# Another order of the pieces within one period of a software-pipelined graph network on one core

## The chip, the core and the metric

The kernel runs on one core of one Trainium2 chip. TensorE (PE) multiplies matrices into PSUM, of which the kernel uses eight banks; VectorE (DVE), ScalarE (ACT) and GpSimd (POOL) do the elementwise work; SyncE (SP) issues the DMA transfers. Each engine works through its own queue in order, and semaphores make one engine wait for another. The metric is the device time in microseconds of one launch, lower is better.

## What is computed

64 graphs of 256 nodes with 256 features, all in fp32, through two layers. `adj` holds 0 and 1. Layer 0 is graph attention (twice), LayerNorm, and a feed-forward block with relu:

```python
def _gat(h, adj, W, a, out_features):          # twice
    Wh = h @ W
    e = leaky_relu(Wh @ a[:out] + swap(Wh @ a[out:]), 0.2)
    return softmax(where(adj > 0, e, NEG), axis=1) @ Wh
h = _layernorm(x + _gat(_gat(x, adj, W1, a1), adj, W2, a2), g_ln1, b_ln1)
x = _layernorm(h + relu(h @ w_ff1 + b_ff1) @ w_ff2 + b_ff2, g_ln2, b_ln2)
```

Layer 1 is attention with 8 heads whose weights are split by relation, then LayerNorm and a feed-forward block with gelu (256 to 1024 to 256, as in layer 0):

```python
attn = softmax(q @ k.T / sqrt(32))
for r in range(4):
    out = out + (attn * (adj == r)) @ (x @ Wv[r] + bv[r])
x = _ln(x + out @ Wo + bo, g1, beta1)
return _ln(x + gelu(x @ W1 + b1) @ W2 + b2, g2, beta2)
```

## The kernel before

**Pieces.** `binary` (L211) does all the work; `general` (L1181) stands behind a test at the end and handles adjacency values other than 0 and 1, which this input doesn't have. For each graph `graph` (L1126) fills a table of small functions, the *pieces*, of one to 64 instructions each. Their names have a stage and a step:

- L: loads of one graph. L.xT (columns of x), L.adj (L363) and L.x (rows of x, L373), 256 KB each.
- G, graph attention (`gat`, L824): projections wh0, wh1 on TensorE and their copies wc0, wc1 on ScalarE; for each of the two steps A and B the transposed targets e, terms lr, masked maximum ad (L893 to L899, VectorE), exponentials ex, normalisation rz; the products gA0, gA1 with copies wd0, wd1, and the second product gB. Then LayerNorm A: lnA, rsA, nmA.
- F: the features of layer 0's first LayerNorm are turned into columns (dtA on VectorE, dmA and mgA on SP, see below), feed-forward block, LayerNorm B (lnB, rsB, nmB), columns again (dtB, dmB, mgB), and the queries and keys.
- A: the values of layer 1, scores sc0, sc1, maxima mx, exponentials ex, reciprocals rz, normalisation sp (POOL), the turning of the weights over DRAM (dt, dm, mg), masks pm (L1071, VectorE), products o0, o1 and their copies oc0, oc1.
- T: the output projection wo, LayerNorm C, the second feed-forward block, LayerNorm D, and the store T.out.
- S and W occur at the start alone (weights, and matmuls that warm up TensorE).

**Seven products.** A product of 2 x 2 blocks is done with seven block products instead of eight (`seven_products`, L692). It appears four times for each graph: h, the hidden layer of a feed-forward block (`into`, L758); f, its output (`out_of`, L796); q, queries and keys (L967); v, values (L991). TensorE's part is five pieces: `a` (products X and Z, two PSUM banks), `b` (Y, a third bank), `c` (adds to X and to Y), `d` and `e` (add to X). The running values of X are taken out between them by k1 to k4, and Z and Y are added by p1, p2, p3:

```python
for piece, f, *args in (
    ("k1", keep, "X", 0, 0), ("p1", plus, "Z", 0, 0), ("k2", keep, "Y", 1, 1),
    ("k3", keep, "X", 0, 1), ("p3", plus, "Y", 0, 1), ("p2", plus, "X", 1, 1),
    ("k4", keep, "X", 1, 0),
):
```

For h, k1 to k4 are copies on ScalarE (L770) and p1 to p3 additions on VectorE (L734); for f both are on VectorE (L809 and L734); for q, k is on ScalarE (L984) and p on VectorE (L988); for v, k1 and k4 are copies on ScalarE or VectorE additions of a bias (L1006), and p VectorE additions. The four sums of blocks that the products need are POOL's (`add_sums`, L676): F.sA, F.sB, T.sC for columns, one piece each; F.u0 to F.u3 and T.u0 to T.u3 for the hidden layer, one sum each, into a tile H of which there is one. So the names read thus: F.fc is the third TensorE piece of layer 0's output product, F.u3 the POOL sum that its second half needs, F.fk3 the VectorE instruction that takes X out after it. In the profile, tiles of layer 0's feed-forward block end in `_a` (hX_a, fZ_a, acc_a, cols_a), those of layer 1's in `_c`, queries and keys are qX, qY, qZ, and cols_y, S_y are their columns and sums. F.r0 to F.r3 and T.ge0 to T.ge3 are the activations of the hidden layer (L776, ScalarE).

**LayerNorm.** `layernorm` (L562): statistics on VectorE (ln), the power -0.5 on POOL (rs; with two further small POOL instructions, L587 the last, where `scalar` is set, as in LayerNorm B), the normalised rows on ScalarE or VectorE (nm). POOL then multiplies with the gain (ra, L629) and adds the bias over a 128x512 tile (rb, L634).

**Turning.** `turned` (L533) transposes 32x32 squares on VectorE (dt, L542), writes them to DRAM with one DMA (dm, L546) and reads them back as columns with four (mg, L553). All are on SP's queue, and dm waits for dt there.

**The order.** Nothing is scheduled automatically. Inside `tc.manual_schedule` (end of `binary`) every engine's queue holds its instructions in the order in which the pieces are called. The list START runs once, then the list PERIOD 58 times, then END. An entry `F.fc/3` of PERIOD runs piece F.fc for the graph that is 3 behind the newest, so a period has pieces of seven graphs:

```python
for period in range(lags, B):
    for piece, lag in order:
        run(piece, period - lag)
```

An entry's place among entries of other engines has no effect by itself; its place among those of its own engine (or of SP, for its DMAs) is its place in that queue. The calls do allocate tiles, however: `mm_tile` (L233) takes the next of eight PSUM banks, and a new tile waits for the readers of the one whose bank it gets. TensorE's order in a period before is: F.fb G.eB F.fc G.wh1 F.fd A.va F.fe T.fd G.gB T.ha A.vb T.hb T.hc T.hd G.eA A.vc T.he A.vd G.wh0 T.fe F.qa F.qb A.ve F.qc F.ha F.qd F.hb F.qe A.sc1 F.hc F.hd T.fa T.fb F.he A.o1 A.o0 A.sc0 T.wo G.gA1 T.fc F.fa G.gA0.

Of the kernel before, what the change touches and what calls it, by code (L numbers as in the profile page):

```python
# [42 lines left out]


PERIOD = """
A.ex03/4 F.fb/3 G.wd0/2 A.rz03/4 F.u3/3 F.fp1/3 F.fk2/3 G.eB/2 F.u2/3 A.sp02/4 F.fc/3 A.mx00/4
A.mx01/4 G.wh1/1 F.fk3/3 G.lrB/2 G.adB/2 F.fd/3 F.fp2/3 A.sp03/4 A.dt01/4 A.dm10/4 A.ex00/4
A.ex01/4 G.exB/2 T.u2/6 A.rz00/4 G.rzB/2 A.va/4 F.fp3/3 F.fe/3 T.dmC/5 T.raC/5 F.fk4/3 T.fd/6
T.mgC/5 F.lnB/3 L.xT/0 G.gB/2 T.ha/5 G.wc1/1 F.rsB/3 A.pm12/4 T.sC/5 A.vk1/4 A.rz01/4 A.vb/4
F.nmB/3 T.hk1/5 G.lnA/2 T.hb/5 F.dtB/3 T.hk2/5 G.rsA/2 T.hp1/5 A.sp01/4 A.dm01/4 T.hc/5 A.mg10/4  # L50
T.hk3/5 G.nmA/2 F.raB/4 F.dtA/2 T.hd/5 A.vk2/4 G.most/1 T.hp3/5 G.eA/1 T.hp2/5 T.ge0/5 F.dmB/3
F.dmA/2 T.fp2/6 A.sp00/4 A.vc/4 A.vp1/4 T.rbC/5 A.vk3/4 T.he/5 A.pm13/4 F.mgB/3 A.vp3/4 A.pm10/4
F.sB/3 G.lrA/1 F.mgA/2 A.vd/4 A.pm11/4 T.ge1/5 G.wh0/0 T.hk4/5 T.fe/6 G.wc0/0 F.qa/3 T.ge2/5
F.qk1/3 A.vp2/4 A.dt00/4 F.qb/3 A.ve/4 F.qk2/3 G.adA/1 F.qc/3 F.qk3/3 F.qp1/3 F.sA/2 F.ha/2 F.qp3/3
T.ge3/5 G.exA/1 F.qd/3 F.qp2/3 T.fk4/6 A.vk4/4 T.u0/5 F.hb/2 F.qe/3 A.mg01/4 F.hk1/2 A.sc1/3
T.lnD/6 F.hp1/2 A.mx11/3 F.hk2/2 A.dm00/4 A.pm03/4 A.mg00/4 T.u1/5 A.mx13/3 F.hc/2 A.mx10/3 F.hk3/2
A.ex13/3 A.mx12/3 T.rsD/6 L.adj/0 F.hp3/2 F.qk4/3 F.hd/2 A.pm02/4 F.hp2/2 A.ex12/3 A.pm01/4
A.rz13/3 T.fa/5 T.nmD/6 A.pm00/4 F.r1/2 T.fb/5 F.he/2 T.u3/5 A.rz12/3 A.o1/4 A.sp12/3 A.ex10/3
A.ex11/3 A.o0/4 T.rbD/6 F.hk4/2 F.r0/2 A.sp13/3 A.oc1/4 L.x/1 A.sc0/3 A.rz10/3 A.oc0/4 T.out/6
A.rz11/3 G.rzA/1 F.rbB/4 A.dt11/3 F.r3/2 A.sp11/3 T.fk2/5 T.wo/4 F.r2/2 T.fk1/5 G.away/0 T.fp1/5  # L60
G.gA1/1 A.sp10/3 A.mx03/3 A.dm11/3 F.raA/2 G.wd1/1 F.rbA/2 A.mx02/3 T.fc/5 T.lnC/4 T.fk3/5 A.dt10/3
A.ex02/3 T.fp3/5 T.rsC/4 F.fa/2 G.gA0/1 A.mg11/3 F.u0/2 T.nmC/4 F.u1/2 T.dtC/4 F.fk1/2 A.rz02/3
""".split()


# [1416 lines left out]
```

## Time and profile before

| | |
|---|---|
| median of 3 runs | 2996.35 us |
| the runs | 2993.79, 2996.35, 2996.53 us |
| the profiled execution | 2993.21 us |
| its span | 2991.4 us |
| mean granted TensorE clock | 0.995 |
| VectorE's masks L1071 | 512, 708 ns each |
| transposes L542 of 128x1024 | 256, 1232 ns each |
| POOL's sums S_y, L676 | 128, 518 ns each |
| DMA | 449.27 MB, 150 GB/s |

The span goes from the first to the last instruction that the profiler recorded; the execution's own time is 1.8 us more. The page gives for each engine the time it was busy, then the chain of work that ended last, followed back from the end of the run from each instruction to what released it. The same chain can be read in order of time, with a start, a duration and a count of instructions to a row; a list of waits gives what each engine waited for, in total, in number and the longest; and a timeline gives each instruction with its start and its duration. Ends of matmuls are modelled, so that a TensorE row that follows another without a break may include a short wait. A matmul's row in the timeline is longer than its place in the queue, since matmuls overlap; the start of the next row tells how long TensorE was taken. The numbers of a period stand for one of the 58; a period lasts 45.12 us (median).

### The profile page before, as it was taken

How to read it: one execution, taken by the hardware profiler on the slowest of the kernel's cores; microseconds unless marked ns; L12 is line 12 of the kernel's file. 1: busy time of each engine (PE TensorE's matmuls, PEld its weight loads, DVE VectorE, ACT ScalarE, POOL GpSimd, SP SyncE). 2: the span in 40 equal slices, each digit the busy share in tenths (PEclk: the TensorE clock that was granted, in tenths of full speed). 3: DMA queues.
4: the chain of work that ended last, by engine and by line, in shares of the span. 5: the costliest groups of instructions: out<-in, count | busy, mean ns of one | idle time of the engine just before them, and what ended most of it. 6: DMA issues, size and time to landing. Idle time of an engine off the chain costs nothing.

```text
span 2991.4 us, 75422 instructions
## 1 busy us (share of the span) xinstructions
PE 2947.1 (99%) x25662; PEld 2672.7 (89%) x25662; DVE 2599.5 (87%) x6247; ACT 2232.7 (75%) x6404; POOL 2281.8 (76%) x3455
## 2 busy tenths in 40 slices
PE   8999999999999999999999999999999999999997
PEld 7889999989999999999899899999999998898985
DVE  4888888888889888888898898898888898888885
ACT  3677787787787777777777777777877877877764
POOL 6777777777777777777778778777777787777785
PEclk9999999999999999999999999999999999999999
DMA  5545445445445444444444454454454444444442
GB/s 140 156 149 160 149 150 155 155 146 159 150 152 158 148 149 155 149 152 155 151 155 153 153 156 150 152 159 145 150 161 150 149 158 150 147 158 148 135 156 86
DMA packets 401891, 449.27 MB, mean 150 GB/s; under 512 B 41152, under 2 KB 342720, under 8 KB 401504
## 3 DMA queue, kind: packets, MB, share of 16 engines
q1 hardware_dynamic: 399984, 442.14, 46.7%
q8 instruction: 209, 3.42, 0.5%
q0 software_dynamic: 976, 1.72, 0.3%
q14 instruction: 178, 1.46, 0.2%
q10 hardware_dynamic: 544, 0.52, 0.1%
HBM read 242.90 MB, written 201.33 MB: 148 GB/s over the span
## 4 chain that ended last, share of the span: by engine, by line
PE 90%; POOL 3%; DVE 2%; DMA 2%; issue 1%; SPq 1%; ACT 0%; POOLq 0%; DVEq 0%; ACTq 0%
PE hX_a L758 8%; PE o L1082 8%; PE fX_a L796 7%; PE fX_c L796 7%; PE hX_c L758 7%; PE sc L1024 5%; PE wo L1103 4%; PE hY_a L758 4%; PE qX L967 4%; PE fY_c L796 4%; PE hY_c L758 4%; PE fY_a L796 3%; PE gat_a L930 3%; PE gat_b L930 3%; PE wh L847 3%; PE vX L991 3%
## 5 line engine op out<-in xcount | busy, mean ns | idle before, releaser
L1071 DVE SCALAR_TENSOR_TENSOR pm<-away,pm 128x512 f32<-128x512 uint8 x512 | 356.8, 708 | 4.4 <-DMA pm<-far_p 4.0
L542 DVE STREAM_TRANSPOSE p<-p 128x1024 f32<-128x1024 f32 x256 | 315.4, 1232 | 4.1 <-POOL p L1057 4.1
L1082 PE MATMUL o<-pm,v 128*32 128x256 f32 x4096 | 235.9, 381 | 0.0
L776 ACT ACTIVATE hid_c<-hid_c,col_L_gnn_b 128x256 f32<-128x256 f32 x512 | 231.5, 505 | 1.8 <-DVE hid_c L734 0.4
L776 ACT ACTIVATE hid_a<-hid_a,col_L_gnn_b_ff 128x256 f32<-128x256 f32 x512 | 224.2, 501 | 2.4 <-DVE hid_a L734 2.2
L796 PE MATMUL fX_a<-f_L_gnn_w_ff,hid_a 128*128 128x128 f32 x1536 | 203.8, 276 | 1.7 <-DVE acc_a L734 1.3
L796 PEld LDWEIGHTS fX_a<-f_L_gnn_w_ff,hid_a 128*128 128x128 f32 x1536 | 196.0, 192 | 10.5 <-DVE acc_a L734 2.4
L796 PE MATMUL fX_c<-f_L_gnn_W,hid_c 128*128 128x128 f32 x1536 | 203.5, 275 | 0.8 <-DVE acc_c L734 0.4
L1082 PEld LDWEIGHTS o<-pm,v 128*32 128x32 f32 x4096 | 126.6, 110 | 85.7 <-DVE pm L1071 1.1
L796 PEld LDWEIGHTS fX_c<-f_L_gnn_W,hid_c 128*128 128x128 f32 x1536 | 191.8, 192 | 5.6 <-DVE acc_c L734 0.6
L676 POOL TENSOR_TENSOR S_y<-cols_y 128x128 f32<-128x128 f32 x128 | 66.3, 518 | 121.1 <-DMA cols_y<-far_y_y 120.8
L770 ACT COPY hid_a<-hX_a 128x512 f32<-128x512 f32 x192 | 113.1, 589 | 60.5 <-PE hX_a L758 60.2
L1024 PE MATMUL sc<-kT,qT 32*128 32x256 f32 x2048 | 146.7, 400 | 2.5 <-DVE kT L988 2.4
L864 ACT COPY wh_B<-gat_a 128x258 f32<-128x258 f32 x124 | 46.3, 374 | 133.5 <-PE gat_a L930 133.5
L758 PE MATMUL hX_a<-S_a,f_L_gnn_w_ff 128*128 128x128 f32 x1024 | 144.1, 284 | 0.0
L758 PEld LDWEIGHTS hX_c<-cols_c,f_L_gnn_W 128*128 128x128 f32 x1024 | 131.0, 191 | 13.1 <-DVE hid_c L734 3.1
L758 PEld LDWEIGHTS hX_a<-S_a,f_L_gnn_w_ff 128*128 128x128 f32 x1024 | 124.0, 191 | 19.7 <-issue 19.2
L758 PE MATMUL hY_c<-S_c,f_L_gnn_W 128*128 128x128 f32 x1024 | 139.5, 279 | 0.0
L758 PE MATMUL hX_c<-cols_c,f_L_gnn_W 128*128 128x128 f32 x1024 | 135.3, 275 | 2.9 <-DVE hid_c L734 2.5
L796 PE MATMUL fY_a<-f_L_gnn_w_ff,H_a 128*128 128x128 f32 x1024 | 137.3, 277 | 0.8 <-DVE acc_a L809 0.6
L796 PE MATMUL fY_c<-f_L_gnn_W,H_c 128*128 128x128 f32 x1024 | 136.0, 276 | 1.5 <-POOL H_c L676 0.9
L758 PE MATMUL hX_a<-cols_a,f_L_gnn_w_ff 128*128 128x128 f32 x1024 | 136.0, 276 | 0.4 <-DMA cols_a<-far_y_a 0.3
(2844 smaller groups left out, 10562.5 us busy)
## 6 DMA issues: line engine op xcount, KB each, us to landing
far_p<-p SPq DMA_DIRECT2D x256, 512.0 KB, 3.0
pm<-far_p SPq DMA_DIRECT2D x1024, 128.0 KB, 3.0
adj<-in_adjT SPq DMA_DIRECT2D x64, 256.0 KB, 3.4
far_y_a<-sq_a SPq DMA_DIRECT2D x64, 256.0 KB, 2.1
cols_a<-far_y_a SPq DMA_DIRECT2D x256, 64.0 KB, 2.0
far_y_y<-sq_y SPq DMA_DIRECT2D x64, 256.0 KB, 2.0
cols_y<-far_y_y SPq DMA_DIRECT2D x256, 64.0 KB, 2.0
far_y_c<-sq_c SPq DMA_DIRECT2D x64, 256.0 KB, 2.0
```

The costliest lines, as they stand in the source:

```text
L542: nc.vector.transpose(to, rows)
L758: nc.tensor.matmul(ps[:, f * P : (f + 1) * P], weights()[0][:, factor, f * P : (f + 1) * P], left, start=start and f == 0, stop=f == FC // ...
L770: nc.scalar.copy(hidden(i, h), ps.rearrange("p (f n) -> p f n", n=P))
L776: nc.scalar.activation(tiles["hid"][:, f, :], tiles["hid"][:, f, :], func, bias=b1[:, f : f + 1])
L796: nc.tensor.matmul(ps, left[:, f, :], weights()[2][:, factor, f * P : (f + 1) * P], start=start and f == 0, stop=f == FC // 2 - 1, skip_gr ...
L847: nc.tensor.matmul(t["whp", j], tiles["xT"][:, c, nodes(j)], wx[:, c, :], start=(c == 0), stop=(c == KC - 1),)
L930: nc.tensor.matmul(ps, t["s"][:, j, nodes(i)], t["whz"][:, j, :width], start=(j == 0), stop=(j == NT - 1),)
L967: nc.tensor.matmul(ps[:, nodes(n)], w[:, factor, :], right, start=start and n == 0, stop=n == 1, skip_group_check=True,)
L1024: nc.tensor.matmul(t["sc", g, hh][:, i, :], qkv["q"][hd, g, nodes(i)], qkv["k"][hd, g, :], start=True, stop=True,)
L1071: nc.vector.scalar_tensor_tensor(pm[:, 1], tiles["away"].rearrange("p (a n) -> p a n", a=4), 0.0, pm[:, 0], ALU.is_equal, ALU.mult,)
L1082: nc.tensor.matmul(ps[hh * DH : (hh + 1) * DH, :], qkv["v"][:, j, d0 : d0 + DH], t["pm", (g, hh)][:, r].rearrange("p a (j t r) -> p j t a ...
L1103: nc.tensor.matmul(t["wo"][:, i, :], t["oT"][:, c, nodes(i)], late["wo"][:, c, :], start=(c == 0), stop=(c == KC - 1),)
```

## The change

Only the list PERIOD is written in another order. It has the same entries with the same lags, and START and END, the pieces, the tile sizes and the numbers of buffers are the same.

```diff
--- before.py
+++ after.py
@@ -43,23 +43,23 @@
 
 
 PERIOD = """
-A.ex03/4 F.fb/3 G.wd0/2 A.rz03/4 F.u3/3 F.fp1/3 F.fk2/3 G.eB/2 F.u2/3 A.sp02/4 F.fc/3 A.mx00/4
-A.mx01/4 G.wh1/1 F.fk3/3 G.lrB/2 G.adB/2 F.fd/3 F.fp2/3 A.sp03/4 A.dt01/4 A.dm10/4 A.ex00/4
-A.ex01/4 G.exB/2 T.u2/6 A.rz00/4 G.rzB/2 A.va/4 F.fp3/3 F.fe/3 T.dmC/5 T.raC/5 F.fk4/3 T.fd/6
-T.mgC/5 F.lnB/3 L.xT/0 G.gB/2 T.ha/5 G.wc1/1 F.rsB/3 A.pm12/4 T.sC/5 A.vk1/4 A.rz01/4 A.vb/4
-F.nmB/3 T.hk1/5 G.lnA/2 T.hb/5 F.dtB/3 T.hk2/5 G.rsA/2 T.hp1/5 A.sp01/4 A.dm01/4 T.hc/5 A.mg10/4
-T.hk3/5 G.nmA/2 F.raB/4 F.dtA/2 T.hd/5 A.vk2/4 G.most/1 T.hp3/5 G.eA/1 T.hp2/5 T.ge0/5 F.dmB/3
-F.dmA/2 T.fp2/6 A.sp00/4 A.vc/4 A.vp1/4 T.rbC/5 A.vk3/4 T.he/5 A.pm13/4 F.mgB/3 A.vp3/4 A.pm10/4
-F.sB/3 G.lrA/1 F.mgA/2 A.vd/4 A.pm11/4 T.ge1/5 G.wh0/0 T.hk4/5 T.fe/6 G.wc0/0 F.qa/3 T.ge2/5
-F.qk1/3 A.vp2/4 A.dt00/4 F.qb/3 A.ve/4 F.qk2/3 G.adA/1 F.qc/3 F.qk3/3 F.qp1/3 F.sA/2 F.ha/2 F.qp3/3
-T.ge3/5 G.exA/1 F.qd/3 F.qp2/3 T.fk4/6 A.vk4/4 T.u0/5 F.hb/2 F.qe/3 A.mg01/4 F.hk1/2 A.sc1/3
-T.lnD/6 F.hp1/2 A.mx11/3 F.hk2/2 A.dm00/4 A.pm03/4 A.mg00/4 T.u1/5 A.mx13/3 F.hc/2 A.mx10/3 F.hk3/2
-A.ex13/3 A.mx12/3 T.rsD/6 L.adj/0 F.hp3/2 F.qk4/3 F.hd/2 A.pm02/4 F.hp2/2 A.ex12/3 A.pm01/4
-A.rz13/3 T.fa/5 T.nmD/6 A.pm00/4 F.r1/2 T.fb/5 F.he/2 T.u3/5 A.rz12/3 A.o1/4 A.sp12/3 A.ex10/3
-A.ex11/3 A.o0/4 T.rbD/6 F.hk4/2 F.r0/2 A.sp13/3 A.oc1/4 L.x/1 A.sc0/3 A.rz10/3 A.oc0/4 T.out/6
-A.rz11/3 G.rzA/1 F.rbB/4 A.dt11/3 F.r3/2 A.sp11/3 T.fk2/5 T.wo/4 F.r2/2 T.fk1/5 G.away/0 T.fp1/5
-G.gA1/1 A.sp10/3 A.mx03/3 A.dm11/3 F.raA/2 G.wd1/1 F.rbA/2 A.mx02/3 T.fc/5 T.lnC/4 T.fk3/5 A.dt10/3
-A.ex02/3 T.fp3/5 T.rsC/4 F.fa/2 G.gA0/1 A.mg11/3 F.u0/2 T.nmC/4 F.u1/2 T.dtC/4 F.fk1/2 A.rz02/3
+G.wd0/2 F.u3/3 A.mx00/4 G.eB/2 F.u2/3 F.fb/3 F.fk2/3 F.fc/3 G.lrB/2 F.fp1/3 A.ex03/4 F.fk3/3
+G.adB/2 A.dm10/4 T.u2/6 F.fd/3 A.sp02/4 T.dmC/5 A.rz03/4 F.fp2/3 A.mx01/4 G.wh1/1 A.ex00/4 A.va/4
+G.exB/2 F.fe/3 T.raC/5 A.vk1/4 A.sp03/4 G.rzB/2 F.fp3/3 T.fd/6 F.fk4/3 T.mgC/5 G.wc1/1 F.lnB/3
+T.rbC/5 F.rsB/3 G.gB/2 A.dt01/4 A.rz00/4 G.most/1 A.ex01/4 F.nmB/3 G.lnA/2 L.xT/0 A.rz01/4 T.sC/5
+A.vb/4 T.ha/5 A.mg10/4 F.dtB/3 T.hk1/5 G.rsA/2 F.raB/4 T.fp2/6 A.vk2/4 A.dm01/4 T.hb/5 G.nmA/2
+T.hk2/5 F.dmB/3 T.hc/5 F.dtA/2 A.vp1/4 T.hk3/5 T.hp3/5 T.hd/5 T.hp2/5 A.pm12/4 F.dmA/2 T.hp1/5
+A.vc/4 A.sp01/4 T.ge0/5 F.rbB/4 A.vk3/4 G.eA/1 A.sp00/4 A.pm13/4 F.mgB/3 A.vp3/4 T.he/5 G.lrA/1
+A.pm10/4 T.fe/6 A.vd/4 T.hk4/5 F.mgA/2 T.ge1/5 F.sB/3 G.wh0/0 A.vp2/4 F.qa/3 F.qb/3 A.mg01/4
+T.ge3/5 A.dt00/4 A.ve/4 G.adA/1 F.qk1/3 F.qk2/3 A.dm00/4 A.mg00/4 F.qc/3 A.pm11/4 A.vk4/4 F.qk3/3
+G.wc0/0 T.ge2/5 F.sA/2 F.hb/2 F.qd/3 T.fk4/6 F.qp2/3 F.ha/2 F.qp3/3 G.exA/1 F.qp1/3 T.u0/5 F.qe/3
+F.hk1/2 T.lnD/6 A.sc1/3 A.pm03/4 A.mx10/3 F.hk2/2 F.qk4/3 A.mx12/3 F.hc/2 T.rsD/6 T.fb/5 A.mx13/3
+A.mx11/3 A.ex10/3 F.hk3/2 F.hp3/2 F.hd/2 T.fa/5 A.pm02/4 F.hp2/2 A.pm01/4 T.fk2/5 A.ex12/3 T.nmD/6
+A.ex11/3 A.ex13/3 F.he/2 T.u1/5 A.rz12/3 A.o1/4 A.oc1/4 F.hk4/2 T.rbD/6 A.pm00/4 A.sp12/3 A.rz13/3
+A.rz10/3 A.sp13/3 T.u3/5 A.rz11/3 F.hp1/2 T.fk1/5 F.r0/2 A.sp10/3 L.adj/0 A.o0/4 T.out/6 A.oc0/4
+A.sc0/3 A.dt11/3 G.rzA/1 F.r3/2 G.away/0 T.wo/4 T.fp1/5 A.mx02/3 F.raA/2 T.fc/5 A.mx03/3 A.dm11/3
+F.r1/2 F.rbA/2 F.r2/2 A.mg11/3 A.sp11/3 G.gA1/1 A.ex02/3 T.lnC/4 F.u0/2 T.fk3/5 G.gA0/1 T.rsC/4
+F.u1/2 G.wd1/1 T.fp3/5 A.dt10/3 L.x/1 T.nmC/4 F.fa/2 F.fk1/2 A.rz02/3 T.dtC/4
 """.split()
```

TensorE's order in a period after is: G.eB F.fb F.fc F.fd G.wh1 A.va F.fe T.fd G.gB A.vb T.ha T.hb T.hc T.hd A.vc G.eA T.he T.fe A.vd G.wh0 F.qa F.qb A.ve F.qc F.hb F.qd F.ha F.qe A.sc1 F.hc T.fb F.hd T.fa F.he A.o1 A.o0 A.sc0 T.wo T.fc G.gA1 G.gA0 F.fa. On SP's queue L.x has gone from between L.adj and T.out to the end, behind A.mg11; and A.mg10 has gone ahead of A.dm01; the rest of that queue is as before. On POOL's queue T.rbC has gone from behind T.sC to ahead of F.rsB, F.rbB from the end of the period to the middle, and T.rsC behind F.u0. On VectorE's queue A.pm12 and T.hp1 have gone behind T.hp2, T.fp2 and A.vp1 ahead of it.

## The prediction

> **What bounds the kernel.** I began with the engines' shares and the chain that ended last, on the page of the profiled execution.
>
> ```profile
> PE 2947.1 (99%) x25662; PEld 2672.7 (89%) x25662; DVE 2599.5 (87%) x6247; ACT 2232.7 (75%) x6404; POOL 2281.8 (76%) x3455
> ...
> PE 90%; POOL 3%; DVE 2%; DMA 2%; issue 1%; SPq 1%; ACT 0%; POOLq 0%; DVEq 0%; ACTq 0%
> ```
>
> TensorE sets the time, and the other engines matter only where it waits for them. Such waits are mostly too short to show as idle time, because the ends of matmuls are modelled, so I read them from the chain in order of time, in the period from 911 us. A product of eight matmuls of 128x128 takes 0.89 there. Three such products take more:
>
> ```profile
> 932.47 0.94 PE hX_a L758 x8
> ...
> 947.12 0.95 PE fZ_a L796 x8
> ...
> 950.95 0.92 PE fY_a L796 x8
> ```
>
> The first excess, 0.05, is F.hd, which waits for ScalarE's copy F.hk3. The second, 0.06, is F.fa's Z product, whose PSUM bank ScalarE's A.ex02 still reads. The third, 0.03, is F.fc's second half, which waits for POOL's sum F.u3. Two further groups of small waits (T.hc on T.hk1/T.hk2, F.qc on F.qk2) have the same neighbours in both orders. The list of waits adds one that comes now and then:
>
> ```profile
> PE qX L967 <- DMA cols_y<-far_y_y: 5.2, 8, 1.8
> ```
>
> Eight times in the run a transfer comes late to F.qa; 5.2 us in all.
>
> **What the change removes.** No instruction is added or dropped, and every piece keeps its lag; only queue positions differ, in the 58 repetitions of PERIOD.
> - F.hd now stands behind T.fb, 0.89 later: F.hk3 is done by then. F.fa comes last and its Z bank is G.wd1's, read long before. F.u3 no longer has T.rsC between it and its predecessors in time: I add up POOL's rows and find it done 0.7 before F.fc needs it. Together 0.05 + 0.06 + 0.03 = 0.14 a period, 58 x 0.14 = **8 us off**.
> - F.qa's late transfers: between the second attention product G.gB and F.qa stand the same TensorE pieces in both orders, and the chain G.lnA, G.rsA, G.nmA, F.dtA, F.dmA, then F.mgB on SP's queue, is unchanged. SP waits for F.dtA before it may issue F.mgB, as before. So I cost these at no change, between 5 us off (they vanish) and 5 us on (they double, because A.dm01 now goes out behind A.mg10, 2 us before F.dmB).
> - L.x goes from behind L.adj to the end of SP's queue, ahead of A.dm10 and behind A.mg11: 256 KB that G.lnA needs some 12 us later, so free. Should it hold up A.dm10 by its 2 us landing, A.ex00 still has 0.8 us; beyond that each tenth costs VectorE, not TensorE, first.
> - ScalarE's two table loads a period stay two; the longer list of semaphore instructions runs on sequencers ahead of busy engines: nothing.
>
> **What it adds.** F.ha and F.hb change places. In the built program of the changed kernel F.ha's first product, hX_a, gets the PSUM bank that fX_c of T.fe held, and its first matmul waits for T.fk4, the VectorE instruction that empties that bank. Before, F.ha waited for banks emptied early (T.hk4), and T.fk4 had until the scores A.sc1. VectorE's rows in the same period:
>
> ```profile
> 911.70 0.69 DVE L1071 SCALAR_TENSOR_TENSOR pm<-away,pm 128x512 f32<-128x512 uint8 x1
> ...
> 915.39 0.65 DVE L734 TENSOR_TENSOR hid_c<-hid_c,hZ_c 128x512 f32<-128x512 f32 x1
> ...
> 918.85 0.69 DVE L734 TENSOR_TENSOR hid_c<-hid_c,hX_c 128x512 f32<-128x512 f32 x1
> 919.46 0.28 DVE L734 TENSOR_TENSOR acc_c<-acc_c,fX_c 128x128 f32<-128x128 f32 x1
> 919.65 0.41 DVE L734 TENSOR_TENSOR v<-v,vZ 128x256 f32<-128x256 f32 x1
> 919.99 0.42 DVE L1006 TENSOR_TENSOR v<-vX,row_bv 128x256 f32<-128x256 f32 x1
> 920.32 0.76 DVE L1071 SCALAR_TENSOR_TENSOR pm<-away,pm 128x512 f32<-128x512 uint8 x1
> ...
> 926.26 0.28 DVE L988 TENSOR_TENSOR qT<-qT,qZ 128x128 f32<-128x128 f32 x1
> ```
>
> T.hp2 (918.85) is tied to TensorE: it needs T.hd, which ends at the same place after G.gB in both orders. From there VectorE runs without a break to 926.26, 7.41 us. The new order has the same pieces up to T.fk4, with two exchanged: T.fp2 and A.vp1 (919.46 to 919.99, 0.53) have gone ahead of T.hp2, and A.pm12 (from 911.70; the next instruction starts 0.61 later) and T.hp1 (0.65, of which 0.08 overlaps the next) have come behind it, 1.18. So T.fk4 starts 7.41 - 0.53 + 1.18 = 8.06 after T.hp2, at 926.91, and with its 0.28 (as fX_c's other adds here) ends at 927.19.
>
> TensorE's rows:
>
> ```profile
> 925.67 1.06 PE L758 MATMUL hX_a<-cols_a,f_L_gnn_w_ff 128*128 128x128 f32 x8
> ...
> 927.46 0.39 PE L967 MATMUL qX<-S_y,f_Wq 128*128 128x128 f32 x2
> ...
> 927.90 1.06 PE L758 MATMUL hY_a<-S_a,f_L_gnn_w_ff 128*128 128x128 f32 x8
> ```
>
> In the new order F.hb (from 927.90, eight matmuls, 0.89) and F.qd (927.46 to 927.90, 0.44) stand before F.ha, and all the rest before it is the same. TensorE would come to F.ha at 925.67 + 0.89 + 0.44 = 927.00. It is released at 927.19 and some 0.05 (TensorE's start after VectorE's end in its 14 such waits, median): a **new wait of 0.24 in every period** where nothing else made TensorE late. In eight periods F.qa's late transfer covers it: 50 x 0.24 = 12 us. In about a quarter of the periods one of the masks L1071 takes 0.2 more (1.48 for a pair, against 1.28 here): about 3 us. F.hb, now ahead of F.ha, waits for the first sum of F.sA, which ends 0.7 before it in most periods and later in seven; I leave that inside the 3. Sum: **15 us on**. It cannot be below nothing, since a wait gives no time back; its upper bound is T.fk4 0.6 later (three masks slowed by 0.2), 58 x 0.84 = 49, and I take the value of the rows.
>
> Behind F.ha stand F.qe and A.sc1 on TensorE. Their own conditions (F.qp2, F.qp3, F.qp1, G.exA) have ended by then, so the wait is paid once.
>
> A rule to weigh here: mask L1071 reads two SBUF operands. At 920.32 it started while POOL's L634 ran and took 0.76; with POOL idle it takes 0.68. In the new order A.pm12 starts some 0.2 before POOL's F.rbB ends, so it takes the 0.08 and A.pm13 loses it: no change in the sum. The Trainium skill, page "SBUF — State Buffer", section "Who interferes with whom", speaks against this place: such an instruction and a GpSimd one that reads SBUF exclude each other for a whole instruction. By that, A.pm12 would stand about 0.2 longer and the new wait would be near 0.44, some 10 us more.
>
> The Trainium skill, page "Perfetto Trace Analysis", section "Optimization Strategy", says that a gap repeating on the saturated engine can mean too little PSUM for the next tile. That is the kind of wait I expect; the trace of before has none of its size.
>
> **The sum.** The profiled execution took 2993.2 us, 1.8 beyond its span and 3.1 under the median of the three runs, 2996.35. 2993.2 - 8 + 15 = 3000; for the median, 2996.35 + 7 = **3003**, 0.23% slower.
>
> **Rivals.**
> - *VectorE reaches T.fk4 in time* (the other side). Place: T.hp2 to T.fk4; it decides when those 8.06 us are 7.8 or less, for instance because A.pm12 and T.hp1 run 0.24 shorter in their new place. Then only the removals count: 2996.35 - 8 = 2988. Against it: the rows repeat to 0.01 us in most periods.
> - *POOL becomes late.* T.rbC (1.28, L634) moves ahead of F.rsB. I add POOL's rows from F.u0, which must wait for T.fc to free H: T.rbC ends 0.15 before F.rsB may start. F.rsB leads through T.sC, G.rsA, G.nmA, F.dtA to F.mgB and F.qa, and to T.hp2. If POOL's dozen pieces there run 0.35 longer in all (its S_y sum takes 0.69 at one place and 0.44 at another), 0.2 a period go on top: 58 x 0.2 = 12, so 3015. For it: one engine's slack of 0.15; against: POOL's long rows repeat closely.
> - *Nothing to measure.* The two sums cancel within 6 us (0.2% of the time, about what a measurement of this kernel tells from no change): the new wait is 0.05 to 0.23 on average. About 2997.
>
> **Chances.** My forecast with up to some 10 us beyond it, 0.38; POOL late or another wait of that kind, 0.16; nothing to measure, 0.24; VectorE in time, 0.22, since 0.24 of 8.06 is a thin margin for a sum of some sixteen rows. So slower 0.54, same 0.24, faster 0.22. The range goes from VectorE in time with half of F.qa's late transfers gone (2988 - 3) to POOL late with some masks slowed (3015 + 6): 2985 to 3021.
>
> **What would show it.** In the profile of the changed kernel: hX_a from cols_a starts about 0.24 after its predecessor F.qd could hand over, released by VectorE's acc_c L809, in most periods; the rows fZ_a, fY_a and hX_a of F.hd are back to 0.89; F.qa still waits about eight times for cols_y; one period lasts some 0.13 more. It would be wrong if acc_c L809 ended well before hX_a, or if rstd_b L583 followed POOL's L634 without a break.

## The result and the profile after

The changed kernel takes 3004.78 us (median of 8 runs, 3001.87 to 3006.15), the kernel before 2996.02 (8 runs, 2990.35 to 2996.76). The ratio is 1.0031, with a 95% interval of 1.0021 to 1.0040: slower, by about 9 us. The profiled execution took 3004.62 us; its span is 3002.6, 11.2 more than before's. (Before's profiled execution lies 2.8 under its median, so the spans lie further apart than the medians.)

From the page of the changed kernel, the engines' busy times and the chain that ended last, by engine:

```profile
PE 2951.4 (98%) x25662; PEld 2667.0 (89%) x25662; DVE 2622.8 (87%) x6247; ACT 2232.7 (74%) x6404; POOL 2299.0 (77%) x3455
...
PE 78%; DVE 12%; DMA 3%; issue 2%; SPq 2%; POOL 1%; ACT 1%; DVEq 0%; POOLq 0%; ACTq 0%
```

VectorE's share of the chain has gone from 2% to 12%: the chain now runs back through it in many periods. The rows of the period from 877 us show where. First the chain in order of time (start, duration, what):

```profile
885.78 0.45 PE qX L967 x4
...
886.25 1.16 PE hX_a L758 x8
887.41 0.89 PE hZ_a L758 x8
...
892.71 0.89 PE hX_a L758 x8
...
907.30 0.89 PE fZ_a L796 x8
...
910.20 0.89 PE fY_a L796 x8
```

F.ha's first product, hX_a at 886.25, takes 1.16 where eight such matmuls take 0.89; part of the excess is wait that the modelled ends hide. The three products that were too long before (hX_a of F.hd at 892.71, fZ_a at 907.30, fY_a at 910.20) are back to 0.89. VectorE's timeline of the same period, T.hp2 first, A.pm11 and T.fk4 last:

```profile
877.90 0.69 DVE L734 TENSOR_TENSOR hid_c<-hid_c,hX_c 128x512 f32<-128x512 f32 x1
...
885.32 0.68 DVE L1071 SCALAR_TENSOR_TENSOR pm<-away,pm 128x512 f32<-128x512 uint8 x1
885.91 0.28 DVE L809 TENSOR_TENSOR acc_c<-fX_c,res_c 128x128 f32<-128x128 f32 x1
```

And the weight loads of hX_a (a PEld row: before each matmul TensorE loads its weights; in brackets the idle time before the row and what ended it):

```profile
886.25 0.97 PEld L758 LDWEIGHTS hX_a<-cols_a,f_L_gnn_w_ff 128*128 128x128 f32 x8 [0.22 <-DVE acc_c L809]
```

T.fk4 starts 8.01 after T.hp2 and ends at 886.19; the weight loads and the matmuls of hX_a start at 886.25. The list of waits hides most of this, because modelled ends of matmuls cover short waits:

```profile
PE qX L967 <- DMA cols_y<-far_y_y: 4.9, 7, 2.3
...
PE hX_a L758 <- DVE acc_c L809: 2.5, 11, 0.4
```

So I took each TensorE piece of a period from its start to the start of the next one, and averaged over 52 of the 58 periods, without the first three and the last three (us per period, mean):

| piece | before | after | difference |
|---|---|---|---|
| F.hd | 0.940 | 0.893 | -0.047 |
| F.fa | 1.845 | 1.783 | -0.062 |
| F.fc | 1.818 | 1.787 | -0.032 |
| piece ahead of F.qa (late transfers) | 0.957 against 0.891 undisturbed | 0.944 against 0.877 | 0.00 |
| F.qd, with the wait ahead of F.ha | 0.447 | 0.650 | +0.204 |
| F.ha | 1.788 | 1.870 | +0.082 |
| F.qc, F.hb | 1.942 | 1.993 | +0.051 |
| whole period | 45.200 | 45.403 | +0.203 |

58 x 0.203 = 11.8 us, which is the spans' 11.2 to within 0.6. (All 58 periods added up differ by 10.4, so the rest of the 11.2 lies outside them.)

### The profile page after: what moved, and what is told of

The parts are those of the page before. It is cut to its first block, busy times and chain, and to the rows that moved or that the text cites. A ratio compares the mean times of both kernels' runs of the same rounds, so it can differ in the third digit from the quotient of the medians.

```text
span 3002.6 us, 75884 instructions
## 1 busy us (share of the span) xinstructions
PE 2951.4 (98%) x25662; PEld 2667.0 (89%) x25662; DVE 2622.8 (87%) x6247; ACT 2232.7 (74%) x6404; POOL 2299.0 (77%) x3455
## 4 chain that ended last, share of the span: by engine, by line
PE 78%; DVE 12%; DMA 3%; issue 2%; SPq 2%; POOL 1%; ACT 1%; DVEq 0%; POOLq 0%; ACTq 0%
PE hX_a L758 8%; PE o L1082 8%; PE fX_a L796 7%; PE fX_c L796 6%; PE sc L1024 4%; PE wo L1103 4%; PE gat_a L930 4%; PE fY_a L796 4%; PE fY_c L796 4%; PE gat_b L930 4%; PE hX_c L758 3%; PE hY_a L758 3%; PE wh L847 3%; PE qX L967 2%; DMA cols_y<-far_y_y 2%; PE vX L991 2%
## 5 line engine op out<-in xcount | busy, mean ns | idle before, releaser
L796 PEld LDWEIGHTS fX_a<-f_L_gnn_w_ff,hid_a 128*128 128x128 f32 x1536 | 195.8, 191 | 10.4 <-DVE acc_a L734 2.2
L1095 ACT ACTIVATE oT<-o,col_bv 128x256 f32<-128x256 f32 x128 | 60.5, 474 | 135.7 <-PE o L1082 135.6
L758 PEld LDWEIGHTS hX_a<-cols_a,f_L_gnn_w_ff 128*128 128x128 f32 x1024 | 124.4, 192 | 14.8 <-DVE acc_c L809 12.7
L758 PE MATMUL hY_a<-S_a,f_L_gnn_w_ff 128*128 128x128 f32 x1024 | 136.5, 276 | 0.6 <-POOL S_a L676 0.6
L758 PE MATMUL hX_c<-S_c,f_L_gnn_W 128*128 128x128 f32 x1024 | 136.8, 277 | 0.0
```

The source lines that it names most:

```text
L758: nc.tensor.matmul(ps[:, f * P : (f + 1) * P], weights()[0][:, factor, f * P : (f + 1) * P], left, start=start and f == 0, stop=f == FC // ...
L796: nc.tensor.matmul(ps, left[:, f, :], weights()[2][:, factor, f * P : (f + 1) * P], start=start and f == 0, stop=f == FC // 2 - 1, skip_gr ...
L1095: nc.scalar.activation(t["oT"][:, g, :], t["op", g], AF.Identity, bias=bv0[:, g : g + 1], scale=1.0)
```

## Experiments

My theory was: the PSUM bank that F.ha's first product gets is emptied by T.fk4, which VectorE reaches late; this costs some 17 us, and the three removed waits give 8 back. Rivals: POOL's moves are the cost; VectorE is late as a whole; the removed waits are no real ones.

**T.fk4 one mask earlier (fk4_early).** Edit to the changed kernel's PERIOD:

```diff
-... F.qc/3 A.pm11/4 ... F.qd/3 T.fk4/6 F.qp2/3 ...
+... F.qc/3 T.fk4/6 A.pm11/4 ... F.qd/3 F.qp2/3 ...
```

> The changed kernel with one piece moved: T.fk4 stands ahead of mask A.pm11 on VectorE's queue, 0.7 us earlier; PSUM banks are given out as in the changed kernel. Theory (F.ha's bank waits for T.fk4): F.ha's mean excess of 0.29 a period goes, 58 x 0.29 = 17 us, so 2988 us, 8 under the kernel before. Rival 1 (the cost is POOL's: sums of F.sA and F.sB late, from T.rbC and F.rbB moved ahead): nothing of that is touched, 3005. Rival 2 (VectorE is late as a whole, and whatever is behind T.fk4 waits next): between, 2997 to 3005, with a new wait at F.qe or A.sc1.

2987.85 us; ratio to the kernel before 0.9974 (0.9964 to 0.9985). The chain of this run, in order of time, at the same place, and its shares by engine:

```profile
882.41 0.45 PE qX L967 x4
882.85 0.89 PE hX_a L758 x8
```

```profile
PE 87%; POOL 2%; DVE 2%; DMA 1%; issue 1%; SPq 1%; ACT 0%; POOLq 0%; DVEq 0%; ACTq 0%
```

hX_a is back to 0.89, VectorE's share of the chain to 2%. The median period is 44.98: before's 45.12 less 0.14. One VectorE instruction of 0.28 us in the wrong place was the whole loss, 17 us of the 3005.

**T.fk4 later, another bank (fk4_late).**

```diff
-... T.fk4/6 F.qp2/3 F.ha/2 ...
+... F.qp2/3 T.fk4/6 F.ha/2 ...
```

> The changed kernel with T.fk4 one place later on VectorE's queue, behind F.qp2 (some 0.7 us later). The banks are given out anew: F.ha gets those of A.vk4 and G.wc0, and fX_c's bank goes to A.sc1. Theory (it is the bank that ties F.ha to T.fk4, not T.fk4's lateness): F.ha doesn't wait although T.fk4 is later; A.sc1 comes over 1 us behind T.fk4; 2988 us. Rival (T.fk4's place in time is what costs, through whatever it holds up): 3005 or up to 0.7 a period more, 3005 + 58 x 0.7 = 3045.

2991.93 us, ratio 0.9983 (0.9974 to 0.9992). F.ha's first product and T.fk4 in the timelines of TensorE and VectorE:

```profile
882.89 1.06 PE L758 MATMUL hX_a<-cols_a,f_L_gnn_w_ff 128*128 128x128 f32 x8
```

```profile
883.57 0.28 DVE L809 TENSOR_TENSOR acc_c<-fX_c,res_c 128x128 f32<-128x128 f32 x1
```

T.fk4 now ends 0.96 after F.ha has started, and F.ha takes 1.787, without any wait. It is the bank that ties them, and the allocator's choice of a bank changes with one place in the list. The median period is 44.98 as in fk4_early; the mean is 0.06 more, mostly from transfers that came late to F.qa (nine waits, 5.7 us, against six, 4.3).

**The mask ahead of T.fk4 twice (mask_twice).**

```diff
+            for _ in range(2 if h == (1, 1) else 1):
                 nc.vector.scalar_tensor_tensor(
                     pm[:, 1], tiles["away"].rearrange("p (a n) -> p a n", a=4), 0.0, pm[:, 0],
                     ...
```

> The changed kernel with mask A.pm11, the VectorE instruction just ahead of T.fk4, done twice (same result): 0.6 to 0.7 us of VectorE more in each period, ahead of T.fk4; banks as in the changed kernel. Theory: F.ha's wait grows by all of it, 0.6 to 0.7 a period, 58 x 0.65 = 38, so 3043 us, a little less in the periods where F.qa came late. Rival (F.ha's wait is not on VectorE, or is covered): 3005.

3081.78 us, ratio 1.0281 (1.0267 to 1.0295), 77 over the changed kernel where 38 were expected. The wait is VectorE's, but its growth has two sizes: 0.75 in the median period, and about 1.9 in 19 of the 58. Here are VectorE and POOL in a period of each kind. First one with a short second mask, at 909.00 (the two masks are one row, x2; the POOL row is T.u0):

```profile
909.00 1.41 DVE L1072 SCALAR_TENSOR_TENSOR pm<-away,pm 128x512 f32<-128x512 uint8 x2
910.33 0.28 DVE L809 TENSOR_TENSOR acc_c<-fX_c,res_c 128x128 f32<-128x128 f32 x1
```

```profile
909.79 1.75 POOL L676 TENSOR_TENSOR H_c<-hid_c 128x512 f32<-128x512 f32 x1 [0.96 <-ACT hid_c L776]
```

Then one with a long one:

```profile
955.08 2.50 DVE L1072 SCALAR_TENSOR_TENSOR pm<-away,pm 128x512 f32<-128x512 uint8 x2
957.51 0.28 DVE L809 TENSOR_TENSOR acc_c<-fX_c,res_c 128x128 f32<-128x128 f32 x1
```

```profile
955.77 1.26 POOL L676 TENSOR_TENSOR H_c<-hid_c 128x512 f32<-128x512 f32 x1 [0.86 <-ACT hid_c L776]
```

In the first period the mask began 0.07 before T.u0: it took 0.69, and T.u0 1.75 instead of 1.26. In the second T.u0 began 0.03 before the mask: T.u0 took its 1.26 and the mask 1.78. Whichever starts first runs, the other stands.

**The same without POOL beside it (mask_twice_u0).** To mask_twice, one move on POOL's queue:

```diff
-... F.qp1/3 T.u0/5 F.qe/3 ... F.hc/2 T.rsD/6 T.fb/5 ...
+... F.qp1/3 F.qe/3 ... F.hc/2 T.rsD/6 T.u0/5 T.fb/5 ...
```

> As mask_twice (mask A.pm11 done twice, same result), with POOL's sum T.u0 moved behind T.rsD, so that no POOL instruction runs beside the second mask. In a third of mask_twice's periods the second mask took 1.7 instead of 0.7 us, and in these T.u0 had started just before it. Theory (the mask stands still until POOL's instruction is over): the long masks go, every period costs the median's 0.76 more than in the changed kernel, 3005 + 58 x 0.76 = 3049. Rival (the long masks have another cause, a DMA or ScalarE): 3082 as mask_twice. T.fb, which needs T.u0, may wait up to 0.15 a period more: up to 9 us on either.

3047.80 us, ratio 1.0185 (1.0170 to 1.0201), the theory's 3049. The mean wait ahead of F.ha falls to its median, and T.fb is late in only two periods, by 0.1. So the long masks were T.u0's doing.

**F.ha and F.hb back in their old order (swap_back).**

```diff
-... F.hb/2 F.qd/3 T.fk4/6 F.qp2/3 F.ha/2 ...
+... F.ha/2 F.qd/3 F.hb/2 T.fk4/6 F.qp2/3 ...
```

> The changed kernel with F.ha and F.hb in their order of before: F.ha ahead of F.qd, F.hb behind it; nothing else moved. The allocator then gives T.he's bank to hX_a and fX_c's bank (emptied by T.fk4) to hZ_a, F.ha's second product. Theory (the bank, not the order, makes the wait): hZ_a is reached 0.45 us earlier than hX_a was in the changed kernel and must still wait for T.fk4, so the wait grows from 0.29 to about 0.8 a period: 2988 + 58 x 0.8 = 3034. Rival (the exchange of F.ha and F.hb is the cost, undoing it undoes the cost): 2988.

3045.42 us, ratio 1.0176 (1.0161 to 1.0192). From the list of waits of TensorE:

```profile
PE hZ_a L758 <- DVE acc_c L809: 28.7, 54, 0.7
```

The wait moved with the bank to F.ha's second product and grew: F.ha takes 2.543 in the median period, 0.76 over its 1.787 (0.8 expected). A further 0.29 a period appears at A.sc1, T.fb and F.hd, which I did not trace. Undoing the visible exchange does not undo its cost: the bank had to be looked up.

**POOL's move undone (rbB_back).**

```diff
-... T.ge0/5 F.rbB/4 A.vk3/4 ... A.sp13/3 T.u3/5 ...
+... T.ge0/5 A.vk3/4 ... A.sp13/3 F.rbB/4 T.u3/5 ...
```

> The changed kernel with POOL's F.rbB back in its place of before, behind A.sp13: 1.27 us less of POOL ahead of F.sB and F.sA. Theory (the cost is F.ha's wait for T.fk4): only the small excess of F.qc and F.hb in late periods, 0.05 a period, can go, and some masks run without POOL beside them: 0 to 6 us off, 2999 to 3005. Rival (POOL's moves are the cost of the change): back to 2988 to 2990.

3024.48 us, ratio 1.0110 (1.0094 to 1.0125): both were wrong. F.ha's wait is there as before (F.qd +0.025), and a new one of 0.29 stands ahead of F.fb, with 0.12 more in F.fb and F.fd. TensorE's timeline at the start of a period:

```profile
1140.51 0.38 PE L870 MATMUL e_B<-ident,wh_B 128*128 128x128 f32 x2
1141.02 1.13 PE L796 MATMUL fY_a<-f_L_gnn_w_ff,H_a 128*128 128x128 f32 x8
```

The two transposes of G.eB take 0.22, and fY_a starts 0.51 after the first. Its bank is the one that T.nmC reads; T.nmC, which T.rsC on POOL released at 1139.84, ended at 1140.87. In this order POOL runs nearly without a break from A.sp10 to T.rsC, and T.rsC ends 0.6 later than in the changed kernel. So F.rbB's new place isn't part of the loss; in the new order it is needed.

**The three removals alone (old_removals).** To the kernel before:

```diff
-... F.hd/2 ... T.fb/5 ... G.gA1/1 ... G.wd1/1 ... T.fc/5 ... T.rsC/4 F.fa/2 G.gA0/1 ... F.u0/2 ...
+... T.fb/5 F.hd/2 ... T.fc/5 G.gA1/1 ... G.gA0/1 G.wd1/1 F.fa/2 ... F.u0/2 T.rsC/4 ...
```

> The kernel before with the three small removals alone: T.fb ahead of F.hd, T.fc ahead of G.gA1 and G.gA0 ahead of F.fa (with G.wd1 behind A.ex02), T.rsC behind F.u0. F.ha, F.hb and T.fk4 stay where they were. Theory: F.hd -0.05, F.fa -0.06, F.fc -0.03 a period, 58 x 0.14 = 8 us off 2996, 2988 us. Rival (such waits are artefacts of how the ends of matmuls are modelled, or come back one piece later): 2996.

3045.21 us, ratio 1.0161 (1.0147 to 1.0175). The three pieces lose exactly what they should (F.hd -0.047, F.fa -0.063, F.fc -0.032), but the list of waits has a new first row:

```profile
PE gat_a L930 <- ACT p L1045: 39.9, 58, 0.9
```

G.gA0 has taken over the bank that F.fa used to get, and waits 0.85 for A.ex02, with 0.10 more in itself: the kernel before has A.ex02 behind T.lnC on ScalarE. The moves of the other engines that I had taken for unrelated are the other half of the removal.

**With A.ex02 in its new place (old_three).** As old_removals, and:

```diff
-... A.mx03/3 ... A.mx02/3 ... T.lnC/4 ... A.ex02/3 ...
+... A.mx02/3 A.mx03/3 ... A.ex02/3 T.lnC/4 ...
```

> The kernel before with the three small removals, and with what G.gA0's bank needs in its new place: as old_removals, and besides A.ex02 ahead of T.lnC (on ScalarE's queue) and A.mx02 ahead of A.mx03 (on VectorE's), as the changed kernel has them. In old_removals TensorE waited 0.85 us and 0.10 more in every period at G.gA0, whose bank A.ex02 frees only after T.lnC. Theory (that wait is A.ex02's place; the three removals are real and additive): the new wait goes, F.hd, F.fa and F.fc keep their gains, 58 x 0.14 = 8 us under the kernel before, ratio 0.9973. Rival (G.gA0 or its neighbours are late in the old order whatever A.ex02 does): slower than before, 1.003 or more.

2988.32 us, ratio 0.9974 (0.9964 to 0.9984); the three pieces have lost 0.047, 0.062 and 0.030, and no piece has become longer by more than 0.012 in the mean (F.qc, a few late periods). The removals are real, and they add up to the 8 us.

**A version that should beat both (avb_later, avp1_last).** Edits to the changed kernel; avp1_last differs only in A.vp1:

```diff
-... A.vb/4 T.ha/5 ... A.vk2/4 ... T.hb/5 ... F.dtA/2 A.vp1/4 ... T.hp2/5 ... A.vk3/4 ... A.dt00/4 ... T.fk4/6 ...
+... T.ha/5 ... T.hb/5 A.vb/4 ... F.dtA/2 A.vk2/4 ... T.hp2/5 A.vp1/4 ... A.vk3/4 ... T.fk4/6 A.dt00/4 ...
```

> A version that should beat both: the changed kernel with T.fk4 ahead of A.dt00 on VectorE (as fk4_early, some 3 us earlier still), and A.vb behind T.hb on TensorE, so that A.vb's 0.43 us cover T.hc's waits for T.hk1 and T.hk2; on VectorE A.vk2 goes behind F.dtA and A.vp1 behind T.hp2. Theory (each small wait of TensorE in a period adds 58-fold, and only those): fk4_early's 2988 less T.hc's 0.11 a period, 58 x 0.11 = 6, so 2982. Rival (T.hc's excess is no wait but how the matmuls are shaped, or A.vb's later end holds up VectorE and T.he): 2988 or more.

avb_later took 2986.52 us, ratio 0.9978 (0.9969 to 0.9987): no better than fk4_early, where 2982 was expected. T.hc lost 0.086, but T.hd gained 0.046 and A.vd 0.101. In TensorE's timeline A.vd's first matmul is the row vX at 1102.24:

```profile
1102.24 0.70 PE L991 MATMUL vX<-f_Wv,S_y 128*128 128x256 f32 x2
1102.77 1.04 PE L847 MATMUL wh<-wx,xT 128*128 128x260 f32 x4
```

The next piece starts 0.54 after it instead of 0.43. A.vk3, which A.vd needs, ended 0.055 ahead of A.vd: nothing was idle for long, and still a tenth of a microsecond is gone.

> As avb_later, with A.vp1 one place later on VectorE's queue, behind A.vk3. In avb_later T.hc lost 0.086 of its excess, but T.hd gained 0.046 (ScalarE's T.hk3 ended 0.11 ahead of it) and A.vd 0.101 (A.vk3 pushed back by A.vp1, ending 0.06 ahead of it, an idle time of nearly nothing). Theory (a release that comes less than some 0.15 us ahead of a matmul already costs up to 0.10): A.vd's 0.10 goes, T.hd's stays; 0.04 a period under fk4_early, 58 x 0.04 = 2 us, ratio to the kernel before 0.996 to 0.997. Rival (A.vd's 0.10 comes from the matmul shapes or the new bank): as avb_later, 0.998.

avp1_last took 2987.50 us, ratio 0.9971 (0.9962 to 0.9980), at the edge of what was expected. A.vk3 now ends 0.45 ahead of A.vd, and A.vd's 0.101 is gone in every period; T.hd keeps its 0.047. The median period is 44.95, the shortest of all, but F.qc was late in a few periods of the profiled execution (up to 2.21 for its 1.05), and I have not found out why. fk4_early, old_three and avp1_last all beat both kernels, by about 0.3% and 0.6%; these runs don't tell them apart.

## Why the prediction was right, and where it was off

- **What is removed: right.** 0.14 a period, 8 us, was predicted; 0.141 was measured, and 0.139 in old_three.
- **F.qa's late transfers: right.** Eight waits of 5.2 us before, seven of 4.9 after.
- **The new wait: right in place, cause and size.** T.fk4 was to start 8.06 after T.hp2, and TensorE to arrive 8.15 after it; the medians are 8.08 and 8.16. It was to wait 0.24 in 50 periods; it waited 0.25 on average in 46. With the masks' lengthened rows, which I had at 3 us, that makes 58 x 0.200 = 11.6 against the 15 of the sum.
- **What the sum left out.** F.ha itself became 0.08 longer, 58 x 0.081 = 4.7 us: the matmul behind a late release costs more than the idle time. I had seen the same excess (F.hd's 0.05) and called it a wait. And F.qc and F.hb gave 0.05 a period in a few late periods, 58 x 0.05 = 3 us; the prediction had F.hb's part of it inside the masks' 3 and F.qc's, two thirds, not at all. So 15 on became 19 on; the smaller wait and the two extra terms partly cancel, so that the sum came out closer than its terms.
- **The sum.** 8 off and 15 on gave 7; the medians give 8.8, the profiled periods 11.8.
- **Rival "VectorE in time":** it became late by what the rows said; fk4_early makes it come true, at the 2988 that the rival named.
- **Rival "POOL late":** T.rbC ended 0.21 ahead of F.rsB (0.15 predicted), and nothing followed from it. What I did not see is that POOL is as tight at the end of the period: rbB_back, with POOL's old place in the new order, costs 20 us.
- **The rule of the Trainium skill, page "SBUF — State Buffer", section "Who interferes with whom": the page was right and my reading of the row wrong.** I read the mask at 920.32 (0.76 instead of 0.68) as a mild slowing. In the kernel before POOL's row beside it is:

```profile
919.25 1.28 POOL L634 TENSOR_TENSOR res_c<-res_c,row_L_gnn_beta 128x512 f32<-128x512 f32 x1
```

It ends at 920.53, so it had 0.21 left when the mask began. In the changed kernel the three masks that began with more than 0.15 of an L634 left took that rest and 0.55, and the 58 that began with as much of an L676 left took the same in the median; so did, in the median, the 61 masks of the kernel before that began during an L634. 0.21 + 0.55 is the 0.76. The mask stands for the rest of POOL's instruction, as the page says, up to 1.1 us in mask_twice. It cost nothing here because A.pm12 began only 0.05 before F.rbB ended.
- **Undoing part of an order** went wrong twice (old_removals, rbB_back), for one reason: I followed the engine that I moved and not who gets the bank next.

## What to carry to other kernels

In a kernel whose bounding engine is full, go through every instruction that it issues in a period and ask who empties its buffer; one late instruction of 0.28 us on another engine cost 17 us here because it came back 58 times. Read which tile gets whose bank from the built program, after every edit: exchanging two pieces, or moving a third, gives the banks out anew, and a wait goes with the bank, not with the piece. A release has to come with a margin: let it end 0.2 us or more ahead of the matmul, not just in time.

## What the runs showed of the hardware

When a matmul needs a buffer that another engine empties, its weight load waits for the release too. That is in the PEld rows: the first weight load of F.ha's hX_a starts 0.05 after T.fk4's end, and the second matmul of the product 0.215 after that load, so 0.27 after the release. Without a late release the second matmul follows 0.112 behind the first. F.hd in the kernel before shows the same with no idle time at all. Here are the matmuls of F.hd (hX_a) and of the product ahead of it (hY_a), then their weight loads:

```profile
1021.64 1.06 PE L758 MATMUL hY_a<-S_a,f_L_gnn_w_ff 128*128 128x128 f32 x8
1022.53 1.10 PE L758 MATMUL hX_a<-S_a,f_L_gnn_w_ff 128*128 128x128 f32 x8
```

```profile
1021.53 0.97 PEld L758 LDWEIGHTS hY_a<-S_a,f_L_gnn_w_ff 128*128 128x128 f32 x8
1022.48 0.97 PEld L758 LDWEIGHTS hX_a<-S_a,f_L_gnn_w_ff 128*128 128x128 f32 x8
```

The loads of hY_a start 0.11 ahead of its matmuls; those of hX_a, 0.05 after the end of F.hk3 on ScalarE, only 0.05 ahead. Measured, as the lead from the releasing instruction's end to the first matmul's start, and the excess of the time from the first matmul's start to the next product's:

| lead, us | excess, us | where |
|---|---|---|
| 0.055 | 0.10 | F.ha in the changed kernel, 46 periods; A.vd in avb_later |
| 0.096 | 0.06 | F.fa's Z product before |
| 0.107 to 0.108 | 0.047 | F.hd before; T.hd in avb_later and avp1_last |
| 0.125 | 0.033 | F.ha, one period; F.fc's Y product before (0.127, 0.03) |
| 0.138 | 0.019 | F.ha, one period |
| 0.144 | 0.073 | T.hc's Y product (released by T.hk2), before and after |
| 0.17 and more | 0.00 | F.ha, ten periods; T.hd before (0.215) |

So a release without any idle time can cost up to a tenth of a microsecond, which a list of waits does not show. Two places differ. At T.hc a semaphore instruction of 0.05 stands ahead of the weight load, which starts 0.113 after the release instead of 0.05; the 0.215 behind it is the same. At A.vd, whose matmuls have 256 columns and follow each other every 0.218, the second matmul starts 0.32 after the first weight load. And an excess of 0.10 is no proof of a late release: F.hc's first product, behind the scores A.sc1, has it in every period of both kernels, though in the kernel before its last release (F.hk1) came 0.65 or more ahead; what holds its weight load back there I have not found out.

A VectorE mask of two SBUF operands and a POOL tensor_tensor over SBUF exclude each other for a whole instruction, in both directions: 0.68 became 1.78, and 1.26 became 1.75 in mask_twice, according to which began 0.03 to 0.07 earlier. POOL's instructions on 128x2 (L586) beside it changed nothing: 58 masks of the kernel before began during one and took 0.68.
